# A graph network's edge loop: a PSUM bank for the sums, node blocks in smaller parts, and another way of shrinking the pipeline's lags

## The chip, the cores and the metric

The kernel runs on one core of one Trainium2 chip. The metric is the device time of one execution in microseconds; smaller is better. Before the change the median of three timed runs is 2609.36 us (2591.1 to 2622.12). One more execution, taken with the hardware profiler, gives the trace; it took 1999.2 us.

The core's engines run their own instruction queues in order and wait for one another through semaphores: TensorE (PE; its weight loads are shown apart as PEld), VectorE (DVE), ScalarE (ACT), GpSimd (POOL), and SyncE (SP), which here only issues DMA transfers.

## The reference

There are 12500 nodes with 64 features, and 200000 edges sorted by their destination. Cut to what matters:

```python
def ssp(x):
    return jax.nn.softplus(x) - jnp.log(2.0)
nodes = node_state[edges].reshape(num_edges, -1)          # x[src], x[dst] side by side
gates = ssp(edge_state @ We1 + be1) @ We2 + be2
soft_cutoff = 1.0 - jax.nn.sigmoid(5.0 * (edges_distance - (CUTOFF - 1.5)))
gates = gates * soft_cutoff
h = ssp(nodes @ Wn1 + bn1) @ Wn2 + bn2
messages = h * gates
message_sum = jnp.zeros_like(node_state).at[edges[:, 1]].add(messages)
new_state = node_state + (ssp(message_sum @ Ws1 + bs1) @ Ws2 + bs2)
x = _layernorm(x + new_state)
```

So each edge gathers two rows of x, runs two small networks, and adds its message to its destination's row; then each node runs a network of its own and a layer norm.

## The kernel before

**Groups.** The edges are cut into 391 groups of 512 (two halves of 256). Since they are sorted by destination, each half falls into a window of 42 neighbouring nodes, whose first node (its base) is found in a prologue. The destination's part of the node network is a product with x that the prologue computes once for all nodes and writes to a table in HBM; a group reads 42 rows of it (`wns`), and a one-hot matrix (`onehot`, L209) picks the right row for each edge inside the same matmul.

**What a group goes through.** `gather` (L176): GpSimd fetches 128 rows of x by index, four times a group; in 12 of the groups one of the four is fetched row by row from SP's queue instead (`fetch`). It is called 19 groups ahead, into 25 buffers. `load` puts the group's edge features and table rows on SP's queue, five groups ahead. `transposes` (L217) turns the gathered rows and one-hots over into a PSUM bank `tx`, and `xcopy` (L222) has ACT copy that to SBUF. `layer1_edge` (L226, L228) and `layer1_node` (L233) write the two networks' first layers into `z`, a pair of PSUM banks. `exps` and `logs` (L243, L246) have ACT take Exp and Ln, `softplus` (L251) has DVE clamp. `layer2_edge` (L257, L260) and `layer2_node` (L265) write the second layers into one bank `gh`; `hcut` and `message` (L270, L274) multiply them on DVE. `scatter` (L278) is a matmul of the messages with the one-hots: the sums for the two windows, 42 columns each. `window` (L287) adds them into `sums`, which holds the message sum of all nodes in SBUF, at an address that DVE loads into a register (L284).

**PSUM.** [...] `z` has two buffers of two banks, `gh` two of one, `tx` two of one. The scatter writes into the unused end of the coming group's `z`. 

**Node blocks.** When the groups that can still reach a range of nodes are done (`block_steps` bounds that from the distribution of the destinations), the nodes of that range are finished: `node_block` gives five parts. `hidden` and `clamp` (L306, L314, L315); `logs` and `ssp` (L318 to L322); `layer2` and `center` (L327 to L337); `square` and `variance` (L341 to L346); `root` and `store` (L350 to L360). Each step of the loop takes one part. There are 26 blocks: 212 nodes, 23 of 512, and two of 256.

**The order** is written by hand (`tc.manual_schedule`): every engine executes its instructions in the order in which the Python loop emits them. Step i of the loop (L514 on) works on several groups at once: transposes of group i+3, first layer of i+1, second layer of i−1, scatter and window of i−3. Steps from `both` (12 before the last group) on shrink these distances at once, to finish sooner after the last group has come in: step `both` takes the second layer of two groups and no transposes, the next step scatters three groups. After the loop the last node blocks run side by side.

Of the kernel before, what the change touches and what calls it, by code (L numbers as in the profile page):

```python
# [31 lines left out]

# [19 lines left out]

P = 128
D = 64
# [10 lines left out]
CATCH_UP = 12  # L65
# [7 lines left out]
def node_blocks(N):  # L73

    rest = N - NB
    first = rest % NB
    assert rest > 0 and first % 2 == 0 and first <= HE
    sizes = ([first] if first else []) + [NB] * (rest // NB) + [HE, HE]
    return [(sum(sizes[:i]), n) for i, n in enumerate(sizes)]
# [18 lines left out]
def gnn_resnorm_kernel(ctx: ExitStack, tc: tile.TileContext, a: dict, out: bass.AP, E: int):  # L98
# [24 lines left out]
    def tx_tile():  # L123
        return psum.tile([P, NB], F32, name="tx")

# [25 lines left out]
    half = const.tile([P, 1], F32, name="half")  # L151
    ones3 = const.tile([PIECES, HE], BF16, name="ones3")
# [78 lines left out]
    def layer1_node(g, h):  # L231
        zn = zs[g][:, h, HE * (1 - h) : HE * (2 - h)]
        nc.tensor.matmul(zn, wns[:, g % REST, h, :], xTs[g][:, h], start=True, stop=True, skip_group_check=True)  # L233
# [29 lines left out]
    def layer2_node(g, h):  # L263
        for t in range(2):
            nc.tensor.matmul(ghs[g][:, 1, 2 * t + h, :], ss[g][:, 1 + h, t, :], wn2, start=False,  # L265
                             stop=h == 1 and t == 1, skip_group_check=True)
# [9 lines left out]
    def scatter(g, sc):  # L276
        for t in range(2):
            nc.tensor.matmul(sc, msgs[g][:, 2 * t : 2 * t + 2, :].rearrange("p h f -> p (h f)"),  # L278
                             xgs[g][:, 2 * t : 2 * t + 2, D:DW], start=t == 0, stop=t == 1, skip_group_check=True)
        scs[g] = sc  # L280

    def window(g):
        for h in range(2):
            base = nc.values_load(base_i[0:1, 2 * g + h : 2 * g + h + 1], engines=[DVE], min_val=0, max_val=N - 1,  # L284
                                  skip_runtime_bounds_check_because="it was clamped to these bounds")
            part = sums[h * D : (h + 1) * D, bass.ds(base, W)]
            nc.vector.tensor_add(part, part, scs[g][h * D : (h + 1) * D, h * W : (h + 1) * W])  # L287

    def node_block(first, n, pool):
# [7 lines left out]
        def tile3(name):  # L297
            return pool.tile([P, 2, 2, D], F32, name=name, bufs=2)[:p, :nq]
# [11 lines left out]
        def clamp():  # L310
            t["y"] = tile3("y")
            nc.sync.dma_start(t["y"], x[rows, :].rearrange("(q p k) d -> p q k d", q=nq, k=2))
            t["l"], t["zb"] = (pool.tile([P, HE], F32, name=name, bufs=2) for name in ("l_s", "zb"))
# [19 lines left out]
        def center():  # L333
            nc.vector.scalar_tensor_tensor(t["y"], t["y"], 2.0, t["u"][:, :nq], OP.mult, OP.add)
            mean = small("mean")
            nc.vector.tensor_reduce(mean, t["y"], AX.X, OP.add)
            nc.vector.scalar_tensor_tensor(t["y"], mean.to_broadcast([p, nq, 2, D]), -1.0 / D, t["y"], OP.mult, OP.add)  # L337
# [5 lines left out]
        def variance():  # L343
            t["v"] = small("var")
            nc.vector.tensor_reduce(t["v"], t["y2"], AX.X, OP.add)
            nc.vector.tensor_scalar(t["v"], t["v"], 1.0 / D, EPS, OP.mult, OP.add)  # L346

        def root():
            t["r"] = small("rstd")
            nc.scalar.activation(t["r"], t["v"], AF.Ln)  # L350
            nc.scalar.activation(t["r"], t["r"], AF.Exp, scale=-0.5)

        def store():

            v, r = t["v"], t["r"]
# [3 lines left out]
            nc.vector.tensor_mul(t["y"], t["y"], r.to_broadcast([p, nq, 2, D]))  # L359
            nc.sync.dma_start(out[rows, :].rearrange("(q p k) d -> p q k d", q=nq, k=2), t["y"])  # L360

        def then(f, g):
            def both():
                f()
                g()
            return both

        return [(hidden, clamp), (None, then(logs, ssp)), (layer2, center), (None, then(square, variance)),
                (None, then(root, store))]

    def node_part(part):
        if part[0]:
            part[0](tx_tile())
        part[1]()

    with tc.manual_schedule():
# [4 lines left out]
        with tc.tile_pool(name="prep", bufs=1) as prep:  # L381
# [23 lines left out]
            nc.vector.memset(half, 0.5)  # L405
            nc.vector.memset(ones3, 1.0)
# [40 lines left out]
            nc.vector.tensor_add(brow[:, 1:3, :], brow[:, 1:3, :], ps[:1, : 2 * D].rearrange("o (i d) -> o i d", d=D))  # L447
            pieces = prep.tile([1, PIECES, 4 * D], BF16, name="pieces")
# [43 lines left out]
        with tc.tile_pool(name="finish", bufs=1) as finish:  # L492
            blocks = list(zip(node_blocks(N), block_steps(N, NG)))
            last = NG - 1
            both = last - CATCH_UP
            second, third, ahead = {}, {}, {}
            for i in range(-3, NG + 1):
                groups = [i - 1] if i < both else [i - 1, i] if i == both else [i]
                second[i] = [g for g in groups if 0 <= g < NG]
                groups = [i - 3] if i <= both else [i - 3, i - 2, i - 1] if i == both + 1 else [i - 1]  # L500
                third[i] = [g for g in groups if g >= 0]
                groups = [i + 3] if i < both else [] if i == both else [i + 2]
                ahead[i] = [g for g in groups if g < NG]
            todo, complete = [], 0
# [9 lines left out]
            for i in range(-3, NG + 1):  # L514
                part = todo.pop(0) if todo else None
# [4 lines left out]
                if i < both:  # L520
                    if 0 <= i + 1:
                        zs[i + 1] = z_tile()
                    for g in third[i]:
                        scatter(g, zs[i + 1][:, 1, HE : HE + 2 * W])
                    for g in second[i]:
                        layer2_edge(g)
                elif i + 1 < last:
                    zs[i + 1] = z_tile()
                if i + 1 < last:
                    at(layer1_edge, i + 1)  # L530
                    at(layer1_node, i + 1, 0)
                    at(layer1_node, i + 1, 1)
                if part and part[0] and i + 2 < last:
                    part[0](tx_tile())
                for g in ahead[i]:
                    transposes(g)
                if i + 1 < last:
                    at(exps, i + 1)
                    if i < both:
                        at(logs, i + 1)  # L540
                for g in ahead[i]:
                    xcopy(g)
                if i >= both and i + 1 < last:
                    logs(i + 1)
                if i + 2 == last:
                    zs[last] = z_tile()
                    layer1_edge(last)
                for g in second[i]:
                    if i >= both:
                        layer2_edge(g)  # L550
                    if i + 2 == last:
                        layer1_node(last, 0)
                        layer1_node(last, 1)
                    layer2_node(g, 0)
                    layer2_node(g, 1)
                if i + 2 == last:
                    for some in (edge, node):
                        exps(last, some)
                        logs(last, some)
                if i + 1 < last:  # L560
# [180 lines left out]
```

## Time and profile before

| | |
|---|---|
| timed runs | 2591.1, 2609.36, 2622.12 us |
| profiled execution | 1999.2 us, span from first to last instruction 1997.4 us |
| PE busy | 1881.8 us (94%) |
| PEld busy | 1505.4 us (75%) |
| POOL busy | 1474.1 us (74%), 1551 gathers of 0.95 us |
| DVE busy | 1050.5 us (53%) |
| ACT busy | 919.0 us (46%) |
| mean granted PE clock | 0.986 |

Busy time is the union of an engine's instruction intervals; a group's line in the page gives its operation, its count, its busy time, the mean time of one, and after the second bar the idle time of its engine just before it and what ended that. `issue` there is time in which the engine waited for nothing that the profile shows. PE's fp32 matmuls come as two passes, each with a weight load, so that counts of L233 and others are double those in the source. The granted clock is a share of full speed.

### The profile page before, as it was taken

To read this page: it belongs to the slowest core of one execution; us is meant where nothing else is said; L and a number is where in the kernel's file an instruction comes from. 1 tells how busy PE (TensorE), PEld (TensorE's weight loads), DVE (VectorE), ACT (ScalarE), POOL (GpSimd) and SP (SyncE) were. 2 spreads that over 40 slices of the span, in tenths; PEclk is the share of its full clock that TensorE was granted. 3 is DMA by queue.
4 is the path that set the end of the run, shared out by engine and by line. 5 is a ranking of instruction groups with operands and counts; after the bars stand their busy time and mean duration, and the time that the engine had idled before them with its cause. 6 is when DMAs were issued, how large, how long until landed. Compare 5 with 4: busy or idle time off the path is not lost.

```text
span 1997.4 us, 42101 instructions
## 1 busy us (share of the span) xinstructions
PE 1881.8 (94%) x11378; PEld 1505.4 (75%) x11378; DVE 1050.5 (53%) x2752; ACT 919.0 (46%) x1322; POOL 1474.1 (74%) x1555
## 2 busy tenths in 40 slices
PE   4999999999999999999999999999999999999996
PEld 4888888887777777777777777777777877777775
DVE  4455555555544545545555555555554555555555
ACT  1344545454444444444444444444454554444433
POOL 7777777777777777777777777777777777777770
PEclk9999999999999999999999999999998999999988
DMA  8432222222223223232222322232222232223220
GB/s 231 140 68 68 66 69 68 67 67 69 66 68 69 58 66 69 62 70 61 63 68 64 69 65 64 68 69 69 68 65 68 64 71 68 68 71 68 68 61 25
DMA packets 171021, 143.15 MB, mean 72 GB/s; under 512 B 46507, under 2 KB 142947, under 8 KB 170778
## 3 DMA queue, kind: packets, MB, share of 16 engines
q1 hardware_dynamic: 119778, 87.95, 15.2%
q0 software_dynamic: 49632, 50.92, 14.2%
q8 instruction: 95, 1.56, 0.3%
q10 hardware_dynamic: 1368, 1.51, 0.3%
q14 instruction: 148, 1.21, 0.2%
HBM read 130.57 MB, written 9.63 MB: 70 GB/s over the span
## 4 chain that ended last, share of the span: by engine, by line
PE 58%; DMA 20%; POOL 7%; issue 6%; ACT 4%; DVE 3%; DVEq 1%; POOLq 0%; SPq 0%; ACTq 0%
DMA xg<-in_x,src_i 19%; PE gh L265 11%; PE z L233 9%; PE gh L260 8%; PE z L228 8%; POOL xg L176 7%; PE tx L217 6%; PE z L278 6%; PE gh L257 4%; PE z L226 3%; ACT u L246 2%; ACT u L243 2%; PE z L471 2%; DVE s L251 1%; DVE sums L287 1%
## 5 line engine op out<-in xcount | busy, mean ns | idle before, releaser
L176 POOL DMA_INDIRECT xg<-in_x,src_i x1551 | 1473.9, 950 | 476.8 <-issue 310.0
L251 DVE SCALAR_TENSOR_TENSOR s<-u,z 128x768 f32<-128x768 f32 x392 | 373.2, 952 | 842.6 <-ACT u L246 776.7
L243 ACT ACTIVATE u<-z 128x768 f32<-128x768 f32 x392 | 317.4, 810 | 975.8 <-PE z L233 975.8
L233 PE MATMUL z<-xT,wns 106*128 106x256 f32 x1564 | 410.0, 384 | 0.0
L265 PE MATMUL gh<-consts,s 128*128 128x64 f32 x3128 | 394.1, 269 | 0.0
L265 PEld LDWEIGHTS gh<-consts,s 128*128 128x128 f32 x3128 | 391.6, 196 | 0.1
L246 ACT ACTIVATE u<-u,one 128x768 f32<-128x768 f32 x392 | 366.1, 934 | 12.3
L217 PE MATMUL tx<-consts,xg 128*106 128x128 f32 x1552 | 283.5, 283 | 69.9 <-DMA xg<-in_x,src_i 63.9
L233 PEld LDWEIGHTS z<-xT,wns 106*128 106x128 f32 x1564 | 301.3, 193 | 44.4 <-issue 0.4
L217 PEld LDWEIGHTS tx<-consts,xg 128*106 128x106 f32 x1552 | 194.9, 133 | 164.9 <-DMA xg<-in_x,src_i 116.1
L260 PE MATMUL gh<-consts,s 128*128 128x128 f32 x1564 | 279.9, 301 | 0.0
L228 PE MATMUL z<-eT,consts 128*128 128x256 f32 x782 | 277.9, 437 | 0.0
L260 PEld LDWEIGHTS gh<-consts,s 128*128 128x128 f32 x1564 | 205.1, 191 | 89.0 <-issue 88.3
L278 PE MATMUL z<-xg,msg 128*128 128x84 f32 x1500 | 235.4, 279 | 0.0
L222 ACT COPY xT<-tx 106x512 f32<-106x512 f32 x391 | 221.6, 567 | 9.5 <-PE tx L217 9.1
L278 PEld LDWEIGHTS z<-xg,msg 128*128 128x128 f32 x1500 | 198.1, 192 | 0.0
L270 DVE TENSOR_TENSOR h<-gh,cut 128x256 f32<-128x256 f32 x391 | 166.0, 425 | 14.7 <-PE gh L265 2.2
L274 DVE TENSOR_TENSOR msg<-gh,h 128x256 f32<-128x256 f32 x391 | 166.0, 425 | 13.5
L228 PEld LDWEIGHTS z<-eT,consts 128*128 128x128 f32 x782 | 118.0, 190 | 47.6 <-issue 1.5
L287 DVE TENSOR_TENSOR sums<-sums,z 64x42 f32 x750 | 144.3, 192 | 13.0 <-issue 6.1
L257 PE MATMUL gh<-row,ones 3*128 3x512 bf16 x391 | 150.8, 386 | 0.0
L209 DVE TENSOR_TENSOR xg<-consts,rel 128x168 f32<-128x168 f32 x391 | 126.8, 325 | 1.1 <-issue 0.4
(79 smaller groups left out, 590.9 us busy)
## 6 DMA issues: line engine op xcount, KB each, us to landing
eT<-in_eT SPq DMA_DIRECT2D x391, 128.0 KB
xg<-in_x,src_i POOLq DMA_INDIRECT x1551
xr<-in_x SPq DMA_DIRECT2D x1536, 0.2 KB
wns<-table SPq DMA_DIRECT2D x782, 21.0 KB
table<-tb SPq DMA_DIRECT2D x14, 448.0 KB
sums<-in_xT SPq DMA_DIRECT2D x7, 455.0 KB
y<-in_x SPq DMA_DIRECT2D x23, 128.0 KB
out<-y SPq DMA_DIRECT2D x23, 128.0 KB
```

Source lines behind the costliest of these rows:

```text
L176: nc.gpsimd.indirect_dma_start(out=xg[:, k, :D], out_offset=None, in_=x, in_offset=bass.IndirectOffsetOnAxis(ap=src_i[:, g, k : k + 1], ax ...
L217: nc.tensor.transpose(tx[:, k, :], row, ident)
L222: nc.scalar.copy(xT, xTs[g])
L228: nc.tensor.matmul(zs[g][:, 0, :HE], we1.rearrange("a h d -> a (h d)"), eTs[g], start=False, stop=True, skip_group_check=True)
L233: nc.tensor.matmul(zn, wns[:, g % REST, h, :], xTs[g][:, h], start=True, stop=True, skip_group_check=True)
L243: nc.scalar.activation(us[g][:, part], z_of(g)[:, part], AF.Exp)
L246: nc.scalar.activation(us[g][:, part], us[g][:, part], AF.Ln, bias=one)
L251: nc.vector.scalar_tensor_tensor(ss[g].rearrange("p i t e -> p (i t e)")[:, part], us[g][:, part], BIG, z_of(g)[:, part], OP.min, OP.max)
L257: nc.tensor.matmul(gh, ones3[:, :P], row3.rearrange("q i k d -> q (i k d)"), start=True, stop=False, skip_group_check=True)
L260: nc.tensor.matmul(v[:, 0, t], ss[g][:, 0, t, :], we2, start=False, stop=False, skip_group_check=True)
L265: nc.tensor.matmul(ghs[g][:, 1, 2 * t + h, :], ss[g][:, 1 + h, t, :], wn2, start=False, stop=h == 1 and t == 1, skip_group_check=True)
L278: nc.tensor.matmul(sc, msgs[g][:, 2 * t : 2 * t + 2, :].rearrange("p h f -> p (h f)"), xgs[g][:, 2 * t : 2 * t + 2, D:DW], start=t == 0, s ...
```

## The change

It does four things.

- The scatter gets a PSUM bank of its own (`sc`), and `tx`, which held two, gets one. The scatter moves from the head of a step to its end, after `layer2_node`; `window` follows `message` on DVE, and `softplus` comes after `onehot`. Both bases of a group are loaded into registers by one instruction.
- A node block comes in ten parts over steps 1 to 12 after its sums are complete (three steps for a block near the end), and the fetch of its rows of x comes five groups earlier. Its matmuls write to the free end of `z`. There are 25 blocks: the last 512 nodes are one.
- The layer norm's mean is split: the weights and the bias of the block's second layer have their mean taken out once, in the prologue, and so only the rows of x are centred per block, before the second layer instead of after it. A part of the variance's arithmetic goes to the activation's own scale and bias.
- The lags shrink over the last 14 groups: step 376 scatters two groups and has no transposes, step 377 transposes group i+2, step 378 none, and then each step transposes group i+1 at its head. The last group's work is written out after the loop, with its register loads ahead.

The diff, cut to its core:

```diff
@@
     def tx_tile():
-        return psum.tile([P, NB], F32, name="tx")
+        return psum.tile([P, NB], F32, name="tx", bufs=1)
+
+    def sc_tile():
+        return psum.tile([P, NB], F32, name="sc", bufs=1)
@@
-    def scatter(g, sc):
+    def scatter(g, n):
+        sc = (tx_tile if n else sc_tile)()[:, : 2 * W]
         for t in range(2):
             nc.tensor.matmul(sc, msgs[g][:, 2 * t : 2 * t + 2, :].rearrange("p h f -> p (h f)"),
-                             xgs[g][:, 2 * t : 2 * t + 2, D:DW], start=t == 0, stop=t == 1, skip_group_check=True)
+                             xgs[g][:, 2 * t : 2 * t + 2, D:DW], start=t == 0, stop=t == 1)
         scs[g] = sc
@@
+    def window_bases(g):
+        _, window_at[g] = nc.values_load_multi_w_load_instructions(
+            base_i[0:1, 2 * g : 2 * g + 2], engines=[DVE], min_val=0, max_val=N - 1,
+            skip_runtime_bounds_check_because="they were clamped to these bounds")
@@ node_block
-        return [(hidden, clamp), (None, then(logs, ssp)), (layer2, center), (None, then(square, variance)),
-                (None, then(root, store))]
+        return [Part(None, fetch), Part(hidden, clamp), Part(None, logs), Part(None, center), Part(None, ssp),
+                Part(layer2, add), Part(None, square), Part(None, variance), Part(None, root), Part(None, scale),
+                Part(None, store)]
@@ prologue
+            mean = prep.tile([P, 3], F32, name="mean_w")
+            nc.vector.tensor_reduce(mean[:, :2], ws2, AX.X, OP.add)
+            nc.vector.tensor_reduce(mean[:1, 2:], brow[:, 3, :], AX.X, OP.add)
+            nc.vector.scalar_tensor_tensor(ws2, mean[:, :2].to_broadcast([P, 2, D]), -1.0 / D, ws2, OP.mult, OP.add)
+            nc.vector.scalar_tensor_tensor(brow[:, 3, :], mean[:1, 2:].to_broadcast([1, D]), -1.0 / D, brow[:, 3, :],
+                                           OP.mult, OP.add)
@@ the loop, as it is after
+BLOCK_STEPS = (1, 2, 3, 3, 4, 5, 6, 7, 8, 12)
+BRIEFLY = (1, 1, 1, 1, 2, 2, 2, 3, 3, 3)
+            for i in range(-3, NG):
+                groups = [i - 3] if i < ends else [i - 3, i - 2] if i == ends else [i - 2]
+                third[i] = [g for g in groups if g >= 0]
+                ahead[i] = [i + 3] if i < ends else [i + 2] if i == ends + 1 else [i + 1] if i > ends + 2 else []
...
+                early = i > ends
+                if early:
+                    for g in ahead[i]:
+                        transposes(g)
+                        xcopy(g)
+                at(layer2_edge, i - 1)
+                if i >= -1:
                     zs[i + 1] = z_tile()
+                    layer1_edge(i + 1)
+                    for part in now:
+                        if part.tensor:
+                            part.tensor(zs[i + 1][:, 1, HE:])
+                    layer1_node(i + 1)
+                at(exps, i + 1)
+                at(logs, i + 1)
+                if not early:
+                    for g in ahead[i]:
+                        transposes(g)
+                        xcopy(g)
+                at(layer2_node, i - 1)
+                for n, g in enumerate(third[i]):
+                    scatter(g, n)
+                at(hcut, i - 1)
+                at(message, i - 1)
+                for g in third[i]:
                     window(g)
                 for g in ahead[i]:
                     at(onehot, g + 2)
+                at(softplus, i + 1)
+                for part in now:
+                    part.others()
...
+            begun.pop(2).others()
+            transposes(last)
+            xcopy(last)
+            layer2_edge(last - 2)
+            zs[last] = z_tile()
+            layer1_edge(last)
+            layer1_node(last)
+            for some in (edge, node):
+                exps(last, some)
+                logs(last, some)
+            for g in range(last - 3, last + 1):
+                window_bases(g)
...
+            scatter(last, 1)
+            window(last)
+            for part in begun:
+                node_part(part)
```

## The prediction

> **What bounds the kernel now.** I read the page first, for the busy shares and the costliest groups, then single steps in the timeline.
>
> ```profile
> PE 1881.8 (94%) x11378; PEld 1505.4 (75%) x11378; DVE 1050.5 (53%) x2752; ACT 919.0 (46%) x1322; POOL 1474.1 (74%) x1555
> ...
> L176 POOL DMA_INDIRECT xg<-in_x,src_i x1551 | 1473.9, 950 | 476.8 <-issue 310.0
> ```
>
> PE looks like the bound, but POOL's idle time is not free time: it is 1551 gaps of 0.3 us, one ahead of each gather. So a gather costs 0.95 + 0.30 = 1.25 us and a group, with four, 4.98 us. A PE step that waits for nothing takes less:
>
> ```profile
> 303.36 0.28 PE L226 MATMUL z<-ones,be 3*128 3x256 bf16 x1
> ...
> 307.76 0.28 PE L226 MATMUL z<-ones,be 3*128 3x256 bf16 x1
> ```
>
> That is 4.41 us from one layer-1 start to the next. The twenty groups gathered ahead feed PE until about 480 us; after that its steps average 4.97 us, which is POOL's pace, and the transposes (L217) wait for gathers. The last gather starts late:
>
> ```profile
> 1950.19 0.94 POOL L176 DMA_INDIRECT xg<-in_x,src_i  x1 [0.30 <-DMA xg<-in_x,src_i]
> ...
> 1968.77 0.62 PE L217 MATMUL tx<-consts,xg 128*106 128x128 f32 x4 [0.22 <-PE z L233]
> ...
> 1983.10 0.20 DVE L287 TENSOR_TENSOR sums<-sums,tx 64x42 f32 x1 [0.36 <-DVE sums L287]
> ...
> 1992.39 0.34 SPq L360 DMA_DIRECT2D out<-y  x1
> ```
>
> So of 1997.4 us, POOL sets the first 1951.1. The rest is 46.3 us: gather data landing (about 2.4 us, the pieces of xg in the chain that ended last), 15.3 us in which PE is behind POOL (1953.5 to the last transposes at 1968.8), 14.5 us from there to the last sum, 14.1 us of node block and store. Why PE is behind, busy times by stretch tell (sum and count of PE, PEld, DVE, ACT, POOL, then the granted clock):
>
> ```profile
> 80.00:480.00 400.00, 399.70 (x2531) 328.63 (x2529) 214.32 (x548) 204.13 (x280) 302.73 (x320) 1.00 0.30 69
> ...
> 1917.00:1920.40 3.40, 1.57 (x12) 1.25 (x10) 1.88 (x7) 0.00 (x0) 2.48 (x4) 1.00 0.41 111
> 1920.40:1934.00 13.60, 13.60 (x45) 10.09 (x44) 4.69 (x13) 3.85 (x6) 10.25 (x12) 0.50 0.28 65
> 1934.00:1951.00 17.00, 16.78 (x107) 13.41 (x107) 11.32 (x30) 8.52 (x14) 13.04 (x14) 1.00 0.20 36
> 1951.00:1968.70 17.70, 16.26 (x97) 12.24 (x95) 9.42 (x25) 7.62 (x12) 0.13 (x1) 1.00 0.12 31
> ```
>
> Where the old lags shrink, three scatters queue behind one another's window adds; PE works 1.57 of 3.40 us, and the clock is halved for 13.6 us. Three steps there take 8.39, 8.21 and 7.75 us, 24.35 in all against 14.9 at POOL's pace: 9.4 of the 15.3 us. The scatters themselves:
>
> ```profile
> 1916.74 0.63 PE L278 MATMUL tx<-xg,msg 128*128 128x84 f32 x4
> ...
> 1918.28 0.65 PE L278 MATMUL tx<-xg,msg 128*128 128x84 f32 x4 [0.92 <-DVE sums L287]
> ...
> 1919.85 0.65 PE L278 MATMUL tx<-xg,msg 128*128 128x84 f32 x4 [0.92 <-DVE sums L287]
> ```
>
> [...] six of its seven half-clock stretches last 3.4 or 13.7 us (the seventh runs to the end)[...]. [...] the trace has 0.94 us rows and about 2.4 us more before the reader goes on. [...] the change takes one of the transposes' two away, so the copy L222 must end within a step. In a step at PE's own pace it runs 302.44 to 303.01 and the next transposes begin at 304.96: 1.95 us to spare.
>
> **The change part by part.**
>
> *Bank for sums.* The scatter (four passes, 0.56 us from its start to the next matmul) moves from a step's head to its tail. PE's cyclic order is what it was: L278 was followed by the head L257, and still is. Nothing is removed, so 0. The new wait (scatter on the previous window adds, which end about 1.3 us before the next scatter can start) is covered; uncovered it would cost what the catch-up shows, 0.92 us a step.
>
> *DVE order.* The layer-2 products and window adds (0.42 + 0.42 + 0.40) and the one-hot (0.33) now stand ahead of the softplus (0.95). If PE's second layer is done 2.1 us after its node matmuls start, the softplus ends at 4.95 us and its reader, L260, stands at 7.1: 2.1 us of cover. Queued behind a late window add are the softplus and, through the z bank, the edge matmuls two steps on. Per window pair one register load goes; their adds stand 0.40 us together already: 0 in the loop, but 0.36 us for each of four pairs in the tail.
>
> *Node blocks.* 25 instead of 26, ten parts over twelve steps instead of five over five. A 512 block costs PE 0.86 (four passes of 0.215) + about 0.95 (L327 and L330) = 1.8 us and DVE at most 1.07 us in a step, over a slack of 4.98 − 4.41 = 0.57 us a step: about four steps absorb it, and blocks stand 8 to 43 steps apart. Hidden before and after: 0; if POOL were not the pace, 25 blocks at 1.8 us would lie open in both. The fetch of y (0.41 us of SP's queue) moves five steps ahead, the store to step 12, where its data are long ready, so eT and wns loads behind it wait less. SP issues 2.8 us of DMA a step: covered.
>
> *Means folded.* Four small operations in the prologue, bounded by 0 and 1.2 us (each at most a 0.3 us row as L447); there POOL holds DVE memsets for 14 gathers, so I take 1.0 on the path.
>
> *Lags over 14 groups.* At the shrinking steps 376 to 378 there are two scatters on two banks instead of three; PE then waits about 1.3 us for the transposes' bank. Two steps carry no transposes (0.44 us of PE each). From then on transposes, copy and node matmuls of one group lie in one step: L217 0.44, then edge matmuls of the second and first layer (0.95 + 0.74) cover the copy (0.59). But ACT is a queue: where a brief block's Exp and Ln (0.41 + 0.51) wait for its clamp, which waits for the softplus, the copy waits too. I work out about 1.4 us in the block's second step and 0.8 in its third, plus 1.8 of matmuls: PE is 8.6 us behind POOL after the first brief block, gets back 0.57 a step to 5.8, and is 8 us behind after the second. Bounds: 0 (the copies are never late) and 15.3 (another halved clock). I take 8.
>
> *Tail.* From the last transposes: 0.6, copy 0.6, node matmuls done at 3.4, Exp and Ln in two parts to 6.0, softplus of the node part 7.0; then for the last group products, scatter and window add as rows of before have them (0.42 + 0.42 + 0.60 + 0.40 and hand-overs): last sum at 11.4 against 14.5 before. One block of 512 follows alone: hidden 1.1, clamp 0.5, Exp and Ln 1.0, ssp 0.45, second layer 1.25, add 0.45, square 0.45, reduce 0.45, root 0.45, three small 0.55, scale 0.45, hand-overs 0.7 = 7.8, then store and end 5.0 as before. The last two blocks ran interleaved before, 14.1 with the store; now 12.8.
>
> **Sum.** 1951.1 + 1.0 + 2.4 + 8 + 11.4 + 12.8 = 1986.7 us of span, against 1997.4: −10.7 us, or 0.54%. The profiled execution took 1999.2 us; the three timed runs took 2591 to 2622, 1.305 times as much, and the page doesn't say what is slower in them. If everything is slower alike, 0.54% holds: 2609.36 × 0.9946 = 2595. If only a constant is added, it is 2599.
>
> **Rivals.** (A, likeliest) as summed, 2595; with lag from 0 to 15.3 us in the tail, −19 to −3 us, or 2585 to 2605, and with a spread of runs like that of before (±16) 2570 to 2620.
>
> (B) The timed gap of 610 us is PE at half clock: a step then costs some 8.2 us instead of 4.98, so 190 such steps would fill it. Spread blocks and freed banks leave fewer half-empty windows; with a tenth of these steps gone, 2548. For it: the clock was halved seven times. Against it: a PE that is behind is fully busy, and 80 to 480 us shows no halving at all.
>
> (C) Slower: one mechanism, the transposes' single bank together with the copy's place in ACT's queue. If a block's parts on ACT wait for DVE, the copy is late, the next transposes wait, and PE loses 2.2 us per block. 25 blocks make 55 us, 2664. It decides once PE, not POOL, is the pace, that is, above 4.98 us a step; at POOL's pace the slack hides it. Against it: in the twelve-step spread Exp and Ln stand a step after their clamp.
>
> (D) The change does nothing that shows: the lag stays 15 us and only the tail gains, 3.4 us of 1997.4; 2605.
>
> **How the numbers follow.** A 0.50, B 0.27, C 0.15, D 0.08. 1% is about what a measurement of this kernel can tell from no change. Faster by over 1% (below 2583): most of B and a sixth of A, 0.33. Slower by over 1% (above 2635): C and a little of the spread, 0.16. Within: 0.51. The range 2545 to 2632 leaves out the strong end of B and C; A's own is 2570 to 2620.
>
> **What would show it.** POOL's last gather still starts near 1951 us; 1.25 us from gather to gather; last transposes near 1962 and the last sum 11 to 12 us later; no 3.4 us window at half work near steps 376 to 380; PE's wait for the copies only beside the two brief blocks. I am wrong if the gather pace changes, if steps before 480 us are longer than 4.41 us (then C), or if the clock record of the timed state is what decides (B).

## The result: 1.2% slower

The median of 13 runs is 2618.8 us (2606.0 to 2640.8), against 2599.1 us for 13 runs of the kernel before beside them: a ratio of 1.0121, with an interval of 1.0089 to 1.0153. I had forecast 2595 us, half a per cent faster.

The kernel before took about 2000 us on two chips and about 2600 us on two others, so every ratio compares runs of both kernels on one chip and at one time; "at 2000 us" and "at 2600 us" below name the two kinds by what before took there. The profile that I predicted from was one at 2000 us; the timed runs were at 2600.

From the page of the changed kernel (one execution of 2640.8 us, the longest of the 13; span 2639.0): busy times, the granted clock in 40 slices of the span (in tenths), and the gathers' group.

```profile
PE 2241.8 (85%) x11373; PEld 1786.6 (68%) x11373; DVE 1115.1 (42%) x2745; ACT 919.3 (35%) x1317; POOL 1468.0 (56%) x1555
...
PEclk9998878877888878788888888778888788788876
...
L187 POOL DMA_INDIRECT xg<-in_x,src_i x1551 | 1467.8, 946 | 1013.1 <-issue 371.2
```

POOL's gathers last as before (0.95 us), but it is idle for 1013 us instead of 477; 371 of them are the short gaps that no wait explains, and most of the rest ends with a matmul of PE. From the changed kernel's timeline, a place in the middle and then the lines that answer those of before's end:

```profile
946.87 1.00 PE L279 MATMUL gh<-consts,s 128*128 128x64 f32 x8
...
950.46 0.28 PE L356 MATMUL z<-rs,ones 3*128 3x256 bf16 x1
950.55 0.42 DVE L284 TENSOR_TENSOR h<-gh,cut 128x256 f32<-128x256 f32 x1 [1.63 <-PE z L239]
...
954.97 1.22 PE L359 MATMUL z<-consts,l_s 128*128 128x128 f32 x4 [4.23 <-DVE mean L338]
...
2480.36 0.94 POOL L187 DMA_INDIRECT xg<-in_x,src_i  x1 [0.30 <-issue]
...
2606.89 1.06 PE L228 MATMUL tx<-consts,xg 128*106 128x128 f32 x4
...
2624.99 0.42 DVE L309 TENSOR_TENSOR sums<-sums,tx 64x42 f32 x2 [0.88 <-PE tx L293]
```

The last gather starts at 2480, not 1950, and the last transposes begin 127 us after it, not 19. So PE, not POOL, sets the pace. And PE stands still ahead of a block's second layer (L359): 4.23 us, here between the first of its matmuls (L356) and the rest. What it waits for, from the list of PE's waits (each line: what waits, `<-` what ended the wait, then us in total, times, longest):

```profile
PE z L359 <- DVE mean L338: 81.3, 19, 5.4
PE sc L293 <- PE gh L279: 62.6, 58, 1.4
...
PE tx L228 <- ACT xT L233: 33.2, 7, 24.2
PE gh L273 <- DVE s L264: 27.9, 91, 0.7
...
PE z L359 <- DVE l_s L351: 8.0, 4, 2.8
```

L359 is a node block's second layer, L351 the shifted softplus (`ssp`) that feeds it. L338, the first half of the centring, stands two rows ahead of L351 in the same queue. The wait itself ends with L351: in all 24 blocks of the loop the second layer starts 0.05 to 0.06 us after L351 ends.

### The profile page after: what moved, and what is told of

Read it like the earlier page. It is cut to its first block, busy times and chain, and to the rows that moved or that the text cites. A ratio compares the mean times of both kernels' runs of the same rounds, so it can differ in the third digit from the quotient of the medians.

```text
span 2639.0 us, 41084 instructions
## 1 busy us (share of the span) xinstructions
PE 2241.8 (85%) x11373; PEld 1786.6 (68%) x11373; DVE 1115.1 (42%) x2745; ACT 919.3 (35%) x1317; POOL 1468.0 (56%) x1555
## 4 chain that ended last, share of the span: by engine, by line
PE 79%; DVE 8%; issue 6%; another core or an unknown queue 4%; ACT 1%; DMA 1%; DVEq 0%; ACTq 0%; SPq 0%
PE z L245 16%; PE gh L279 14%; PE z L239 11%; PE gh L273 11%; PE tx L228 9%; PE sc L293 6%; DVE s L264 4%; PE gh L270 4%; PE z L237 3%; PE z L328 2%; DVE xg L220 1%; PE z L359 1%; DVE sums L309 1%; PE z L502 1%
## 5 line engine op out<-in xcount | busy, mean ns | idle before, releaser
L284 DVE TENSOR_TENSOR h<-gh,cut 128x256 f32<-128x256 f32 x391 | 165.8, 424 | 1004.4 <-PE gh L279 398.9
L245 PE MATMUL z<-xT,wns 106*128 106x256 f32 x1564 | 518.7, 462 | 17.6 <-issue 16.3
L279 PE MATMUL gh<-consts,s 128*128 128x64 f32 x3128 | 456.5, 297 | 0.4 <-issue 0.4
L279 PEld LDWEIGHTS gh<-consts,s 128*128 128x128 f32 x3128 | 454.9, 223 | 2.2 <-issue 0.5
L245 PEld LDWEIGHTS z<-xT,wns 106*128 106x128 f32 x1564 | 366.1, 237 | 98.8 <-issue 29.5
L264 DVE SCALAR_TENSOR_TENSOR s<-u,z 128x768 f32<-128x768 f32 x392 | 373.3, 952 | 58.4 <-issue 32.6
L273 PE MATMUL gh<-consts,s 128*128 128x128 f32 x1564 | 320.3, 334 | 35.5 <-DVE s L264 27.9
L228 PE MATMUL tx<-consts,xg 128*106 128x128 f32 x1552 | 289.4, 318 | 62.9 <-ACT xT L233 33.2
L293 PE MATMUL sc<-xg,msg 128*128 128x84 f32 x1552 | 271.5, 302 | 75.9 <-PE gh L279 62.6
L273 PEld LDWEIGHTS gh<-consts,s 128*128 128x128 f32 x1564 | 237.0, 217 | 145.5 <-issue 76.5
L239 PE MATMUL z<-eT,consts 128*128 128x256 f32 x782 | 322.8, 497 | 9.3 <-issue 8.9
L228 PEld LDWEIGHTS tx<-consts,xg 128*106 128x106 f32 x1552 | 228.3, 156 | 135.6 <-issue 47.5
L309 DVE TENSOR_TENSOR sums<-sums,sc 64x42 f32 x776 | 152.5, 196 | 344.3 <-PE tx L228 92.5
L293 PEld LDWEIGHTS sc<-xg,msg 128*128 128x128 f32 x1552 | 228.9, 212 | 84.9 <-PE gh L279 70.9
L233 ACT COPY xT<-tx 106x512 f32<-106x512 f32 x391 | 221.6, 567 | 28.6 <-PE tx L228 9.6
L220 DVE TENSOR_TENSOR xg<-consts,rel 128x168 f32<-128x168 f32 x391 | 130.4, 334 | 14.3 <-issue 2.6
```

The lines of the kernel that those rows point to most:

```text
L228: nc.tensor.transpose(tx[:, k, :], row, ident)
L233: nc.scalar.copy(xT, xTs[g])
L239: nc.tensor.matmul(zs[g][:, 0, :HE], we1.rearrange("a h d -> a (h d)"), eTs[g], start=False, stop=True, skip_group_check=True)
L264: nc.vector.scalar_tensor_tensor(ss[g].rearrange("p i t e -> p (i t e)")[:, part], us[g][:, part], BIG, z_of(g)[:, part], OP.min, OP.max)
L273: nc.tensor.matmul(v[:, 0, t], ss[g][:, 0, t, :], we2, start=False, stop=False, skip_group_check=True)
```

## The theories

A cover is the time by which a result is ready before its reader's turn comes. T1: the change shortened covers between PE and VectorE; at 2600 us PE's signals (the semaphore events with which it tells other engines that a result is there) come late (in the timeline above L284 starts 2.68 us after L279 ends), and the covers do not reach. Candidates are the wait at L359, the scatter's wait for the window adds (single bank), and L273's for the softplus. T2: what costs is the half clock behind PE's half-empty stretches, as in the trace of before, where 1.57 us of work in 3.40 us (from 1917.0) was followed by 13.6 us at a granted clock of 0.50. T3: the prologue or the end.

## The experiments

**Before again, twice at 2000 us and once at 2600 us** (no edit).

> The kernel before, unchanged, against itself. Theory T1 (in the executions that are timed, PE's signals reach the waiting engines up to 4 us late, so the small covers that I costed at nothing lie open): ratio 1.000 within 0.003; the profile's span is near 2600 us, not 1997, the granted clock near 0.83, the time between last gather and end well over 46 us, and PE's steps are longer than 4.41 us although nothing in them is longer. T2 (the granted clock decides): the same span, and the added time lies in stretches at half clock. T3 (the prologue or the tail decides): the span is added there and the steps in the middle stay at POOL's pace of 4.98 us.

> The kernel before, unchanged, once more, for its profile in an execution of the length that is timed. Where before takes about 2600 us: the last gather far past 1950 us (POOL does not set the pace), steps far over 4.98 us, half clock in the range of the changed kernel's 940 us but some 40 to 80 us less of it, and PE gaps over 0.3 us of some 230 us against its 267. Where it takes about 2000 us: as its first profile. Ratio 1.000 within 0.004.

> The kernel before, unchanged, for its profile. Where it takes about 2600 us: the last gather over 2400 us, its steps far over 4.98 us, PE gaps over 0.3 us of 220 to 240 us where the changed kernel has 267 to 286, half clock of 870 to 930 us. Ratio 1.000 within 0.004.

Ratios 0.9991 (0.9969 to 1.0014), 1.0007 (0.9984 to 1.0030) and 0.9990 (0.9954 to 1.0026). The first two were at 2000 us, so what I expected of a 2600 us profile could be compared only with the third. From its page:

```profile
PE 2236.1 (87%) x11378; PEld 1771.5 (69%) x11378; DVE 1045.6 (41%) x2752; ACT 917.7 (36%) x1322; POOL 1472.7 (58%) x1555
...
L176 POOL DMA_INDIRECT xg<-in_x,src_i x1551 | 1472.5, 949 | 952.9 <-issue 379.7
```

So before, too, is not paced by POOL when it is timed. Against the profile that I predicted from, its span is 561 us longer (2558.6 - 1997.4): PE is busy 354 us longer (2236.1 - 1881.8) with the same matmuls, its gaps between matmuls (summed over the trace after 120 us) are 176 us longer (252.6 against 76.9), and the first layer-1 matmul comes 31 us later (107.3 against 76.2). The clock was halved for 880 us against 59. DVE's and ACT's busy times are the same within half a per cent.

What makes gaps shows in VectorE's product L284 after PE's second-layer node matmuls L279. In the timeline of the changed kernel above, L279 ends at 947.87 and L284 starts 2.68 us later, though VectorE was idle for the last 1.63 us of it. The signal is late, not the work. In a run at 2000 us (the five-step blocks, below) the same pair is 0.04 us apart: L279 ends at 891.37, L284 starts at 891.41. The pair is no exception: where VectorE stood idle before L284, the distance has a median of 1.71 us in the changed kernel's profile (377 groups) and of 0.04 us in the five-step run (386 groups).

**A node block's second layer two steps later** (the changed kernel, one line; the four parts behind the second layer move with it):

```diff
-BLOCK_STEPS = (1, 2, 3, 3, 4, 5, 6, 7, 8, 12)
+BLOCK_STEPS = (1, 2, 3, 3, 6, 7, 8, 9, 10, 12)
```

> The changed kernel with a node block's second layer (L359) two steps later after its ssp, nothing else. T1: PE's wait of 81 us at L359 (19 times) goes to under 15 us, and the time falls by 30 to 60 us, to 2560 to 2590 (ratio 0.98 to 0.995). T2: the wait may go, but half clock takes its place elsewhere; ratio 1.005 to 1.015, near 2619. T3: no change, 1.012.

> The changed kernel with a block's second layer two steps later alone. If the wait for the ssp (63 to 81 us) is most of the change's cost: 0.990 to 0.998 at 2600 us; if the scatter's wait is: about 1.008. Where before takes 2000 us it was 1.005.

> The changed kernel with a block's second layer two steps later alone. Where before takes 2600 us: 0.990 to 0.998 if the wait for the ssp (63 to 81 us) is most of the cost, 1.005 to 1.010 if the scatter's wait for the window adds (34 to 63 us) is. Where it takes 2000 us: 1.005 to 1.008 as measured twice.

At 2000 us: 1.0052 (1.0022 to 1.0082) and 1.0077 (1.0049 to 1.0105). At 2600 us: **0.988** (0.982 to 0.994), beside the changed kernel unchanged on the same chip:

> The changed kernel, unchanged. Where before takes 2600 us: 1.010 to 1.014 as measured twice. Where it takes 2000 us: last gather within 3 us of 1950, PE waiting for the ssp 24 times some 1.7 us as in the five-step run, over 200 us at half clock, 50 to 60 us from the last gather to the last transposes instead of my 8 + 2.4; ratio 1.014 to 1.022.

which had 1.0145 (1.0077 to 1.0213). One line turns a slower kernel into a faster one: 2553.0 us against 2615.7. PE's waits in that run, the first two lines of the list and the one for L359:

```profile
PE tx L228 <- ACT xT L233: 54.1, 18, 20.0
PE sc L293 <- PE gh L279: 34.4, 35, 1.4
...
PE z L359 <- DVE l_s L351: 4.0, 2, 2.0
```

The three profiles from this chip, in us:

| | before | changed | second layer later |
|---|---|---|---|
| span | 2558.6 | 2608.6 | 2559.0 |
| PE busy | 2236.1 | 2234.1 | 2209.4 |
| PE gaps after 120 us | 252.6 | 305.5 | 276.4 |
| of them ahead of the block's second layer in the loop | 11.1 | 87.6 | 4.7 |
| half clock after 120 us | 880 | 902 | 848 |

The changed kernel's 50 us over before are gaps: 53 us more of them, PE's busy time alike. The wait ahead of the second layer alone grew by 76. Taking it away gave back 29 us of gaps net (other waits grew, the copy's L228 from 27.7 to 54.1) and 25 us of PE's busy time with the same matmuls, that is, of the clock. Single profiles stand within some 20 us of their medians, and the one of before is 16 us under its own, so the equal spans of before and the later layer don't contradict the ratio of 0.988. The table shows what the later layer takes away from the changed kernel; what makes it faster than before, it does not show.

**Five steps instead of twelve**, at 2000 us:

```diff
-BLOCK_STEPS = (1, 2, 3, 3, 4, 5, 6, 7, 8, 12)
+BLOCK_STEPS = (1, 2, 2, 2, 3, 4, 4, 5, 5, 5)
```

> The changed kernel with a block's eleven parts over five steps as before, instead of twelve, nothing else. T1: the L359 wait stays or grows (its ssp is issued one step earlier still), ratio 1.01 to 1.03. If the spread over twelve steps is itself what costs, the ratio comes back to 1.000. T3: no change, 1.012.

1.0162 (1.0118 to 1.0206). The second layer again stands one step after its ssp, and the wait is there in all 25 blocks. Its timeline shows where the time goes without late signals (L309 window adds, L220 one-hot, L264 softplus of the edges, L338 and L339 centring, L356 and L359 the second layer):

```profile
890.37 1.00 PE L279 MATMUL gh<-consts,s 128*128 128x64 f32 x8
...
891.41 0.42 DVE L284 TENSOR_TENSOR h<-gh,cut 128x256 f32<-128x256 f32 x1 [0.84 <-PE gh L279]
891.87 0.42 DVE L288 TENSOR_TENSOR msg<-gh,h 128x256 f32<-128x256 f32 x1
892.61 0.41 DVE L309 TENSOR_TENSOR sums<-sums,sc 64x42 f32 x2 [0.32 <-issue]
893.05 0.34 DVE L220 TENSOR_TENSOR xg<-consts,rel 128x168 f32<-128x168 f32 x1
893.41 0.95 DVE L264 SCALAR_TENSOR_TENSOR s<-u,z 128x768 f32<-128x768 f32 x1
893.57 0.28 PE L356 MATMUL z<-rs,ones 3*128 3x256 bf16 x1
894.28 0.41 DVE L338 TENSOR_REDUCE mean<-y 128x4 f32<-128x256 f32 x1
894.73 0.42 DVE L339 SCALAR_TENSOR_TENSOR y<-mean,y 128x256 f32<-128x256 f32 x1
895.07 0.42 DVE L351 SCALAR_TENSOR_TENSOR l_s<-zb,l_s 128x256 f32<-128x256 f32 x1
...
895.55 0.74 PE L359 MATMUL z<-consts,l_s 128*128 128x128 f32 x4 [1.70 <-DVE l_s L351]
```

L351 is the last of the step's work on VectorE, behind products, window adds, one-hot, softplus and the centring: it ends 4.1 us after L279. PE gets from there to L359 in 2.5 us, since L359 stands between the edge and the node matmuls of the next step. That leaves 1.70 us, the median of the 25 waits; 42.8 us in all.

In before the ssp was the last of a step's work too, and its reader also came one step later. The same place in the profile that I predicted from (L265 node matmuls, L233 the next step's layer-1 node matmuls, L322 ssp, L327 and L330 second layer):

```profile
890.84 1.00 PE L265 MATMUL gh<-consts,s 128*128 128x64 f32 x8
...
893.94 1.03 PE L233 MATMUL z<-xT,wns 106*128 106x256 f32 x4
...
894.56 0.42 DVE L322 SCALAR_TENSOR_TENSOR l_s<-zb,l_s 128x256 f32<-128x256 f32 x1
894.90 0.28 PE L327 MATMUL tx<-rs,ones 3*128 3x256 bf16 x1
895.11 0.74 PE L330 MATMUL tx<-consts,l_s 128*128 128x128 f32 x4
```

There the ssp ends 3.1 us after the node matmuls, and PE gets to its reader after 3.3 (medians of 24 blocks: 3.08 and 3.34). It was covered, by a quarter of a microsecond. The change puts the centring (L338 and L339, 0.8 us) ahead of the ssp in the same step, and the reader ahead of the layer-1 node matmuls (0.87 us): 4.1 against 2.5. The two together are about the whole 1.7 us; no run moved the centring alone.

The window of 3.4 us that holds the wait is half empty. The same place by stretch (length, busy time and count of PE, PEld, DVE, ACT, POOL, then the granted clock, DMA share, GB/s):

```profile
892.90:896.30 3.40, 1.70 (x9) 1.14 (x9) 2.50 (x6) 0.15 (x1) 2.79 (x3) 1.00 0.30 80
896.30:899.70 3.40, 3.40 (x15) 2.98 (x14) 0.00 (x0) 1.82 (x3) 2.48 (x4) 0.51 0.33 77
899.70:903.10 3.40, 3.40 (x20) 2.63 (x20) 2.55 (x7) 0.40 (x1) 2.48 (x4) 0.99 0.31 77
```

A half-clock stretch begins within -3.0 to +1.3 us of the second layer's start in 21 of the 25 blocks. The run has 217 us of half clock in all, against 59, 108 and 62 in the three profiles of before at 2000 us, and 144 and 161 in the two of the later layer. In the stretches above, 3.40 us with PE busy for 1.70 are followed by 3.40 us at a clock of 0.51. A 1.7 us wait so costs itself and, where such a stretch follows, up to another 1.7 us of PE's work (an estimate: half of the 3.40 us); longer stretches cost more. The 0.57 us of slack a step do not hold that: the last transposes start 53 us after the last gather's end, while that gather still starts at 1951.6.

**Filling the wait** (the changed kernel; the five matmuls' result is overwritten):

```diff
+            for _ in range(5):
+                nc.tensor.matmul(z[:p, :HE], ident[:, :p], consts[:, :HE], start=True, stop=True,
+                                 skip_group_check=True)
             nc.tensor.matmul(z[:p, :HE], ones3[:, :p], rs3..., start=True, ...)
```

> The changed kernel with five idle matmuls (128x256 f32, about 2.2 us in all, their result overwritten) ahead of each block's second layer: PE works while it would wait for the ssp, and the second layer starts no earlier. If the half clock that follows the wait is what costs (T2): half-clock time falls to that of the run with the later second layer (some 145 us), and the ratio to about 1.005 although PE has 25 x 2.2 = 55 us more to do. If the wait itself is what costs (T1): no gain, 1.012 or more.

This was at 2600 us. The changed kernel itself gave 1.0106 on the same chip:

> The changed kernel, unchanged, to stand beside the other runs of this call. Where before takes about 2000 us: its second layers of node blocks wait for their ssp (24 times some 1.7 us as in the five-step run), [...] PE is then 40 to 55 us behind the last gather, which still starts near 1950 us; ratio 1.010 to 1.016. Where before takes about 2600 us: 1.012 as measured first, with some 900 us at half clock.

The filled one gave **0.9958** (0.9924 to 0.9992), 35 us less with 125 matmuls more. From the list of PE's waits in it (L362 is the second layer here):

```profile
PE z L362 <- DVE mean L338: 20.3, 9, 3.1
PE z L362 <- issue: 18.1, 8, 3.3
```

The wait is 41 us with a third entry of 3.1 us (95 in the changed kernel beside it), since part of it is now work; PE's gaps are 259 us against 295. PE's busy time grew by only 6.6 us (2256.0 against 2249.4) although the added matmuls alone take 61 us, and the half clock went from 994 to 813 us. So idling where the second layer waits cost more here than the time that was waited: T2 is right as a part of T1's price, not instead of it.

**Banks and sums' places.** The changed kernel with the banks of before (transposes on two, scatter at the step's head into the layer-1 bank's free end, block matmuls into a transposes' bank after the layer-1 node matmuls):

```diff
-        return psum.tile([P, NB], F32, name="tx", bufs=1)
+        return psum.tile([P, NB], F32, name="tx")
+                if i < ends:
+                    for g in third[i]:
+                        scatter(g, zs[i + 1][:, 1, HE : HE + 2 * W])
                 at(layer2_edge, i - 1)
...
+                for part in now:
+                    if part.tensor:
+                        part.tensor(tx_tile())
```

and the sums' bank cut in halves that scatters take in turn (`sc_bank[:, len(scs) % 2 * HE :][:, :HE]` in place of a new tile), alone and with the later second layer; and banks of before with the later layer.

> The changed kernel with the PSUM banks of before: transposes on two banks, scatters at the step's head in the free end of the layer-1 bank, node blocks' parts in a transposes' bank. If the single banks of sums and transposes are what costs: 1.000 to 1.003. If the spread of the node blocks costs: still 1.010 to 1.016, with PE waiting for the ssp as in the changed kernel.

> The changed kernel with the sums' bank cut in two halves in turn, the second layers where the change has them. If the scatter's wait for the previous window adds (34 to 63 us in the profiles) is what the banks cost, ratio 0.995 to 1.003 at 2600 us. If the later second layer was what helped in the run with both: about 1.010.

> The changed kernel with the second layer of a node block two steps later, and with the sums' bank cut in two halves that the scatters take in turn, so that a scatter waits for the window adds of two groups before it instead of one. If the covers that the change shortened decide (T1), both waits go: ratio 0.995 to 1.003 where before takes 2000 us, under 0.99 where it takes 2600. If the sums' bank costs nothing: as the run with the later second layer alone, 1.005 at 2000 us.

> The changed kernel with the banks of before and the second layer two steps later. If the two effects are separate: near 0.980 at 2600 us (0.9925 less some 0.012) and at or under 1.000 at 2000 us. If they are one (the same half-empty windows): near 0.990.

> The changed kernel with the banks of before and the second layer two steps later. Where before takes 2600 us: 0.970 to 0.980 if the two gains are separate (0.988 and 0.9925 against 1.012 each), near 0.988 if both take away the same half-empty windows. Where it takes 2000 us: 1.007 as measured.

At 2600 us: banks of before 0.9925 (0.9889 to 0.9962), two places with later layer 0.9907 (0.9875 to 0.9938), banks of before with later layer 0.9925 (0.9890 to 0.9961). At 2000 us: two places alone 1.0244 (1.0218 to 1.0271), banks with later layer 1.0070 (1.0032 to 1.0109). Every version in which the second layer stands later is near 0.99, with one bank, two places or the banks of before; adding the banks to the later layer adds nothing, and two places without it leave the wait (43.3 us in 25 blocks) and the loss. The banks run alone, which I had expected at 1.000 or above, does not contradict this, for its edit also moves the block's matmuls behind the layer-1 node matmuls, 0.87 us later in the step, where before has them. Its profile has 38 us of waiting ahead of the second layer, against 95 in the changed kernel beside it, so a good part of its gain is this same wait. It does not show that a single bank costs anything, and the runs do not part what of its gain is the bank and what the place.

**Softplus first on VectorE**, ahead of products, window adds and one-hot, at 2000 us:

```diff
+                at(softplus, i + 1)
                 at(hcut, i - 1)
                 at(message, i - 1)
...
-                at(softplus, i + 1)
```

> The changed kernel with the softplus ahead of the products, the window adds and the one-hot on VectorE, nothing else. T1: PE's wait for the softplus at L273 (28 us, 91 times) goes to under 5 us, but the window adds come 0.95 us later, so that PE's wait at the scatter L293 (63 us) may grow by as much; ratio 0.995 to 1.010. If the order on VectorE is what made the change slower: 1.000 or less. T2 and T3: 1.012.

1.0407 (1.0346 to 1.0468): far worse than either order foreseen. PE's waits in its profile are again the second layer's for its ssp (54.5 us in 25 blocks, median 2.1) and, new, those of a block's first matmuls for the last window adds, 17.5 us in 21 blocks; the scatter, where I had expected a longer wait, does not show in the list. Half clock is 372 us. So the order of the change is the better of the two here; both waits belong to node blocks, and what the later window adds cost shows there and not at the scatter.

**Do gathers hold the signals up?** In the 2600 us profiles PE's signals come in bursts, and in the changed kernel's three profiles the middle half of them comes 1.00 to 1.13 us after the end of a gather behind which POOL stops (more below). A memset of an unused 128x512 tile on GpSimd after the second gather of a group, in the changed kernel and with the later layer:

```diff
             nc.gpsimd.indirect_dma_start(...)
+            if k == 1:
+                nc.gpsimd.memset(idle, 0.0)
```

> The changed kernel with a memset of an unused 128x512 tile on GpSimd after the second gather of each group. If the gathers hold PE's signals up until POOL stops, and other work on POOL lets them through, then where before takes 2600 us the bursts come at the memset too, PE's waits shrink, and the time falls to 2300 to 2500 although POOL has some 200 to 400 us more to do. If only a POOL that waits lets them through, or the gathers have no part in it: 1.01 or more. Where before takes 2000 us POOL is the pace, and the time grows by what the memset adds to a group's 4.98 us, 200 to 400 us.

> The changed kernel with the second layer two steps later and the memset on GpSimd. As the run with the memset alone, less 50 to 60 us where before takes 2600 us; as it, less 20 us, where it takes 2000.

At 2600 us: 1.0138 (1.0071 to 1.0204) and 0.9964 (0.9938 to 0.9990). The memsets took 0.54 us each, 213 us of POOL in all, and the first ratio is that of the changed kernel without them (1.0106 to 1.0145); so POOL has slack there, and other work on POOL in a group's midst does not speed the kernel up. The second is above the 0.988 of the later layer alone, so there they may cost something. The later layer took 40 us off with the memsets in both (2615.5 to 2575.5).

The memset run asked only whether other work on POOL lets the signals through. On whether the gathers have a part in it, the end of the loop says more, where the last gather is past and some twenty groups still pass PE and VectorE. In ten profiles at 2600 us (the changed kernel's three and its variants'), where VectorE stood idle before L284 or its counterpart, it started over 0.3 us after the end of PE's matmuls in 195 to 265 of 314 to 357 groups while gathers ran, and in none of the 18 to 21 groups after the last gather, where it is 0.04 us each time. The waits at L359 follow: in each of the changed kernel's three profiles the last block spread over twelve steps comes behind the last gather and waits 1.7 us, as in the five-step run at 2000 us, while the blocks before it have medians of 4.1 to 4.2. So the late signals go with the gathers under way. By what path, and why at 2600 us alone, stays open: gathers last as long at 2000 us, and in the variants run there this pair is never over 0.04 us apart.

## Why the prediction was wrong

**The gather pace.** "POOL sets the first 1951.1" holds wherever before takes 2000 us: the last gather starts at 1949.4 to 1951.6 in the five variants read there. It does not hold in the timed executions, where it starts at 2424.9 in before and 2480.4 after. I had the warning in hand: the page said 1999, the clock said 2609. "If everything is slower alike, 0.54% holds" was the step that carried the sum over, and everything was not slower alike: DVE, ACT and the gathers lasted the same, and PE had become the pace. The sum of 1986.7 us therefore does not describe the timed executions at all; that the result lies within the stated range of 2545 to 2632 is the width of the range, and not the sum.

**The step that failed: "Hidden before and after: 0" for the node blocks.** I summed PE's and VectorE's work of a block (1.8 and 1.07 us) and set it against POOL's slack. I did not ask when the ssp is ready for its reader. Before had 0.26 us of cover there; the change put the centring ahead of the ssp and the reader ahead of the layer-1 node matmuls, and the cover became a wait of 1.70 us in each block even where signals come at once, 4.2 us (the median) in the timed kind of execution, where they are late. "At most 1.07 us in a step" was wrong too: the step with the centring and the ssp has 0.41 + 0.42 + 0.42 = 1.25 us on VectorE, and this is the step that matters. The durations were in the page of before; the wait was a sum over VectorE's queue against a sum over PE's, as I made it for the softplus in the part on VectorE's order (2.1 us of cover), and left out for the block. The fallback in the same sentence, "25 blocks at 1.8 us would lie open in both", assumed the cost is the same before and after: the wait ahead of the second layer was 11.1 us in before and 87.6 after.

**Rival C** had the sign (2664 forecast, 2619 measured) and the condition (PE, not POOL, as the pace), with a price too high (55 us; the three measurements give 20 to 32), but another mechanism: the copy behind the block's parts on ACT. The transposes waited 33.2 us for copies, 24.2 of them once, at the start of the loop; the remaining 9 us are no match. The block's parts were late, but on VectorE, and PE waited at L359. I had looked at the engine that got a bank less, not at the one whose queue got longer.

**Rival B** was right on what most of the timed gap is, wrong on what the change does to it: 354 of 561 us are PE's longer busy time. The change did not bring the half clock down: it is 902, 919 and 994 us in the three profiles of the changed kernel against 880 in the one of before at 2600 us.

**Bank for sums, VectorE's order: 0.** No run shows a cost of the bank; two places for the sums gained nothing beyond the later layer. At 2600 us PE waits 28 us for the softplus at L273 in 91 pieces of at most 0.7 us: a signal that is 2.7 us late, as in the timeline above, is more than the 2.1 us of cover. **Means folded: 1.0.** The first layer-1 matmul came at 75.3 to 76.5 us in runs of the change's variants at 2000 us against 76.2 to 76.4 in before: nothing measurable in the prologue. What the folding cost stands elsewhere: the centring is now ahead of the ssp.

**Lags and tail: 8 + 2.4, then 11.4 and 12.8.** At 2000 us, with the L359 wait nearly gone, the last transposes start 34.6 and 35.5 us after the last gather's end, not 10.4; before had 17.6, 32.0 and 12.4 in three profiles. The three-scatter stall is gone, but near the end half clock followed on half-empty windows again (0.47 busy ahead of a half-clock stretch at 1922.9 in the first of the runs). From the start of the last transposes to the end of the last sum it then took 18.5 us at half clock, against 11.4 forecast and 14.5 to 15.1 in before. Where the granted clock averaged 0.85 to 0.90 it took 13.5 and 13.0, and from there to the end 13.6 to 14.3 at half clock (forecast 12.8). So the tail's own parts were a little too small, and the lag more than three times too small. At 2600 us 163 us pass from the last gather to the end in the changed kernel and 134 in before beside it, most of it PE's lag (130 and 104 us), while the first layer-1 matmul comes at 107.7 and 107.3: T3's prologue plays no part there either. The longer lag and tail go with the 0.5 to 0.8% that the rest of the change costs at 2000 us where I had −0.54%. The change as it stands was never run at 2000 us; what it does there isn't known beyond its variants.

**What stays open:** by what path signals are late at 2600 us while gathers run, how much of the gain with the old banks is theirs, and why, at 2600 us, the version with the later second layer beats before as well (0.988), while at 2000 us it is slower than before.

## What to carry to other kernels

When work is put ahead of a result in an engine's queue, or its reader moves up in another's, add up both queues to the point where they meet, with the rows of the profile; a free engine does not make the cover, and a result that was in time may have been so by a quarter of a microsecond. If the profiled execution is a quarter shorter than the timed ones, it can have another pace, as here (POOL's at 1999 us, PE's near 2600): count with what the timed one waits for, or let the range say that this is unknown. A wait on TensorE can cost again in clock: in the five-step run 1.70 us of work in 3.40 us was followed by 3.40 us at a clock of 0.51. At 2600 us the reader two steps later took 83 us of such waits away (87.6 to 4.7); other waits grew, and 25 of the 50 us by which the span fell were PE's busy time with the same matmuls. So count the clock beside the gaps.

## What the runs showed that I had not expected

- The same kernel took 30% longer on two chips than on two others, with the same instruction rows: 2600 against 2000 us, mean clock in before's profiles 0.828 against 0.974 to 0.986.
- At 2600 us PE's signals to the other engines bunch. In before's profile they come after a silence of over 1.2 us in 187 bursts of four or more within 0.3 us; in its 2000 us profiles there are none. The middle half of these bursts comes 1.01 to 1.53 us after the end of a gather behind which POOL stops, and POOL's next gather starts 0.26 to 0.63 us later. That alone may say no more than that POOL was waiting for the same signals; that no signal is late after the last gather (0.04 us in all of the 18 to 21 groups there) says that the gathers, or what goes with them, have a part in it.
- Half clock followed on half-empty windows: in the five-step run's block above, 50% busy (1.70 of 3.40 us), then a clock of 0.51. Half-clock stretches in one trace start whole multiples of 3.413 us apart (within 0.02 us for the 7 stretches of the trace that I predicted from and the 84 of the changed kernel's). Cut into such windows, the nine traces at 2000 us show what a window at full clock led to: of those in which PE was busy for at most half, 37 of 38 were followed by half clock; between 0.5 and 0.6, 19 of 27; between 0.6 and 0.8, 53 of 143; above 0.8, 25 of some 4400. So in these traces what a wait costs in clock depends on how it falls into the windows, and no sharp edge shows.
